# An attention and spectral-filter kernel on one core: stores and branch-matrix loads move from GpSimd's queue to SyncE's, with a deeper prefetch and a re-ordered hand-over

## The chip, the core and the metric

The kernel runs on one core of a Trainium2 chip. The core has TensorE (PE, the matrix engine, with its weight loads listed as PEld), VectorE (DVE), ScalarE (ACT), GpSimd (POOL) and SyncE (SP), which only issues transfers. Sixteen DMA engines move data between the core's memory and DRAM. They serve a queue of SP, one of ACT and one of GpSimd. The metric is the device time of one execution in microseconds (us); lower is better. The median of three runs is 2086.2 us (2082.62 to 2087.38).

## The reference, cut to what matters

Two images `x` of 128 channels by 64 x 64 pixels pass two layers, all in float32.

```python
x = x + conv_block(group_norm(x))          # layer 0: 7x7 neighbourhood attention, small linear maps
t = to_tokens(x)                           # (2, 4096, 128)
q = ln(t)
sim = q @ q.T / sqrt(128);  sim[diag] = -1e9
t = t + softmax(sim) @ q                   # layer 1a: attention over each block of tokens
u = ln(t)
# layer 1b ("ffn"): 16 causal filters phi, applied to u and to u with alternating signs,
# times the matrices sum over branches of w_i * M_plus[i], M_minus[i] (each 16 x 128 x 128),
# scaled by sigma**0.25, plus three short lags with M_u
t = t + spectral(u, sigma, phi, M_plus, M_minus) + short_lags(u, M_u)
```

The branch weights `w_i` come from a softmax over four values, and they are the same for all tokens.

## The kernel before, in words

The work runs in five stages, which follow each other on TensorE. Times are those of the profile.

1. **Layer 0**, to 347 us, for both images.
2. **Attention of image 0** (`attention(0, fill)`, L902), 347 to about 788 us.
3. **Attention of image 1** (`attention(1, fill)`), about 788 to 1262 us.
4. **A hand-over**, 1262 to 1314 us, in which the last token chunks of image 1 are finished.
5. **The ffn in frequency space** (`burst`, `project`, `mixed_bins`, `back`, `finished`), 1314 us to the end.

*Attention.* The 4096 tokens of an image are cut into eight chunks of 512. `pairs` (L913) is the list of the 36 chunk pairs, and each pair takes four steps. In a step TensorE makes one 128 x 512 block of scores for the pair that comes next (`weights`, L927), ScalarE takes its exponential (L932), and TensorE multiplies the current block with the tokens of one side (L1054, into the bank `other`). The other side of a pair needs the block transposed. For that the four blocks of a pair, 1 MB, are stored in DRAM by ACT's queue (`sent`, L956, `eb<-e`), loaded back by SP's queue in four pieces of 256 KB (`moved`, L963, `et<-eb`), turned by VectorE in 32 x 32 squares (`turned`, L972) and multiplied (`pair_onto`, L982). The distances are in steps: `MOVE` = 2 for the load, `TURN` = 7 for the turn, `DELAY` = 8 for the multiplication. There are two buffers for `et` and four for `eb`. VectorE must add `other` into `xa` (L1063) before TensorE can start the next pair, because `other` is one bank.

*Filling.* At the end of each step `fill` (L1381) takes one piece of other work from two lists of Python generators. `urgent` holds the chunks whose attention is complete: `after(b, c)` (L1087) normalises a chunk, multiplies it with the transform `tr`, copies the result out on ScalarE (L1128, `uo`), forms sums and differences on GpSimd (L1131, `ub`) and stores them in the DRAM tensor `us` by GpSimd's queue (L1135 and L1140). A chunk makes 16 stores, in three consecutive pieces. `steps` holds the rest: during image 0 the end of layer 0, the branch weights, the filters (`filters`, L1302), whose sums (L1357), negations (L1368) and stores to `gs` (L1332) are all GpSimd's, and the tokens of image 1 (`tokens`, L219); during image 1 `for_ffn` (L1457), which runs `filter_matrices` (L1274), loads `inv` and loads the first four filter blocks (`load_blocks`, L1448).

*`filter_matrices`.* 32 loads of 256 KB (`branch`, L1268, tile `st`, two buffers), each issued by GpSimd one piece ahead of its use. VectorE multiplies each with its branch weight and adds it into `mpl` or `mmi` (L1286, L1288). After every eight loads VectorE forms a difference and a sum (L1294, L1295), and GpSimd scales 8 slices of 128 x 128 by `sigma` (L1298, L1299).

*Order.* From the moment when the buffers of image 1 exist (L1043), the instructions of PE, DVE, ACT and POOL in attention stay in the order in which the program writes them (`manual_schedule`, L1044). SP's stay in the framework's scheduled order, except the four loads of `moved`, which keep their program order. All engines take their queues in order: a waiting instruction holds up everything behind it on its engine.

*Hand-over.* After attention of image 1 what is left in `urgent` is run generator by generator (L1488 to L1493), now with the sums on VectorE and the stores on SP (`adder`, L1484). Some pieces of the short lags (`kept`, L1193, L1209) are mixed in. Then the first four `ut` inputs of the ffn are loaded from `us` (`inputs`, L1520, L1675), and TensorE begins the first `burst` (L1542).

Of the kernel before, what the change touches and what calls it, by code (L numbers as in the profile page):

```python
# [8 lines left out]
F32 = mybir.dt.float32  # L9
# [93 lines left out]
def kernel(  # L103
# [773 lines left out]
    with ap_:  # L877
# [24 lines left out]
        def attention(b, fill):  # L902
# [14 lines left out]
            def weights(a, c, k, left, halves):  # L917
# [32 lines left out]
                    nc.vector.tensor_copy(e[:, 0:lo], pt[:, 0:lo])  # L950
                return e

            def sent(eh):

                eb = dram.tile([P, 4, 512], F32, tag="eb", name="eb", bufs=4)
                nc.scalar.dma_start(out=eb.rearrange("p q r -> p (q r)"), in_=eh)  # L956
                return eb

            def moved(eb):

                et = ep.tile([P, 4, 512], F32, tag="et", name="et", bufs=2)
                for q in range(4):
                    tc.keep_in_program_order(nc.sync.dma_start(  # L963
                        out=et[32 * q : 32 * q + 32], in_=eb[:, q].rearrange("(h p) r -> p h r", h=4)
                    ))
                return et

            def turned(et):

                for q in (0, 2):  # L970
                    flat = et[:, q : q + 2].rearrange("p q r -> p (q r)")
                    tc.keep_in_program_order(nc.vector.transpose(flat, flat))  # L972

            def turned_here(et, es, m):

# [59 lines left out]
            for i, (a, c) in enumerate(pairs):  # L1035
                following = pairs[i + 1] if i + 1 < len(pairs) else None
                coming, halves = [], []
                if a != c:
                    other = ps_o.tile([P, 512], F32, tag="other", name="other")
                else:  # L1040
                    owns[a] = ps_o.tile([P, 512], F32, tag="own", name="own", bufs=2)
                for j in range(4):
                    if tt[1] is not None and not ordered:  # L1043
                        ordered.append(written.enter_context(tc.manual_schedule(engines={engines.PE, engines.DVE, engines.Activation, engines.Pool})))  # L1044
                    if following:
                        coming.append(coming_of(*following, j, coming, halves))
# [35 lines left out]


        spare = [tok[0][:, 0:4, :]]
        adder = [nc.gpsimd, nc.gpsimd]

        def after(b, c):  # L1087

# [35 lines left out]
            def store(pu, n, r0, m, ri):  # L1124

                for s in range(2):
# [5 lines left out]
                    for sgn in range(2):  # L1132
                        to = us[r0 : r0 + m, sgn, :, 2 * hh + s, 2 * fp : 2 * fp + 2, b, par, :]
                        if ri is not None:
                            adder[1].dma_start(  # L1135
                                out=to[:, ri], in_=ub[:, sgn, :].rearrange("p (f d) -> p f d", d=P)
                            )
                            continue
                        for f in range(2):
                            adder[1].dma_start(  # L1140
                                out=to[:, :, f].rearrange("k i d -> i k d"), in_=ub[64 * f : 64 * f + 64, sgn, 0:P]
                            )

            for r0, c0 in row_tiles:
                for ri in range(2):
# [68 lines left out]
        def branch_weights():  # L1214
# [38 lines left out]

            yield
            mu2 = mu.rearrange("p k e -> p (k e)")
            loaded = [branch(m_u, i, nc.sync) for i in range(2)]
            yield
            for i in range(NBR):
                st = loaded.pop(0)
                if i == 0:  # L1260
                    nc.vector.tensor_scalar(mu2, st, wt[:, 0:1], None, ALU.mult)
                else:
                    nc.vector.scalar_tensor_tensor(mu2, st, wt[:, i : i + 1], mu2, ALU.mult, ALU.add)
                yield
                if i + 2 < NBR:
                    loaded.append(branch(m_u, i + 2, nc.sync))

        def branch(src, i, eng):  # L1268

            st = sp.tile([P, 4, P], F32, tag="st", name="st")[:, 0 : src.shape[1]]  # L1270
            eng.dma_start(out=st, in_=src[i].rearrange("k d e -> d k e"))
            return st.rearrange("p k e -> p (k e)")

        def filter_matrices(mpl, mmi):  # L1274

            parts_ = [(k0, dst, src, i) for k0 in range(0, KF, 4) for dst, src in ((mpl, m_plus), (mmi, m_minus)) for i in range(NBR)]
            loaded = [branch(m_plus[:, 0:4], 0, nc.gpsimd)]
            yield
            for at, (k0, dst, src, i) in enumerate(parts_):
                if at + 1 < len(parts_):  # L1280
                    k1, _, src1, i1 = parts_[at + 1]
                    loaded.append(branch(src1[:, k1 : k1 + 4], i1, nc.gpsimd))
                st = loaded.pop(0)
                dst2 = dst[:, k0 : k0 + 4].rearrange("p k e -> p (k e)")
                if i == 0:
# [4 lines left out]
                if dst is mpl or i + 1 < NBR:  # L1290
                    continue
                a, d = (m[:, k0 : k0 + 4, :].rearrange("p k e -> p (k e)") for m in (mpl, mmi))
                s = sp.tile([P, 512], F32, tag="st", name="mdiff")
                nc.vector.tensor_tensor(s, a, d, ALU.subtract)  # L1294
                nc.vector.tensor_tensor(a, a, d, ALU.add)  # L1295
                for k in range(4):
                    ks = slice(k * P, (k + 1) * P)
                    nc.gpsimd.tensor_scalar(a[:, ks], a[:, ks], sg[:, k0 + k : k0 + k + 1], None, ALU.mult)  # L1298
                    nc.gpsimd.tensor_scalar(d[:, ks], s[:, ks], sg[:, k0 + k : k0 + k + 1], None, ALU.mult)  # L1299
                yield  # L1300

        def filters():  # L1302
# [24 lines left out]
            def store(src, r0, n, ri, s, i, o):  # L1327
# [1 line left out]
                    gs.tensor, gs.offset + r0 * 4 * SG * GROW + (i * SG + s) * GROW + o * LL,  # L1329
                    [[4 * SG * GROW, n], [2 * SG * GROW, 2], [1, LL]],  # L1330
                )
                nc.gpsimd.dma_start(out=to, in_=src)  # L1332

            everything = [(r0, c0 + ri * P, (ri,), P) for r0, c0 in row_tiles for ri in range(2)]
            everything.append((left_row, left_col, (0, 1), 64))
# [41 lines left out]
        def filler(b, steps, kept=None):  # L1377
# [3 lines left out]
            def fill(c=None):  # L1381
                if c is not None:
# [7 lines left out]
                        urgent.append(lags)  # L1390
                    return

                for queue in (urgent, steps):
                    while queue:
                        got = next(queue[0], False)
# [31 lines left out]
        for gen in steps:  # L1427
            for _ in gen:
                pass
        mpl, mmi, inv, mu1, ctp = [None] * 5  # L1430

        def blocks(q):

# [11 lines left out]

        first_blocks = []

        def load_blocks():  # L1448
            for q in range(4):
                first_blocks.append(blocks(q))  # L1450
                yield

        def for_lags():
# [2 lines left out]

        def for_ffn():  # L1457

            nonlocal mpl, mmi, inv, mu1, ctp
            while spare != [None]:  # L1460
                yield True
            first_.close()
# [4 lines left out]
            inv = l1.tile([P, K2 // BC * 4 + 1, CQ], F32, name="inv")  # L1467
            ctp = ctx.enter_context(tc.tile_pool(name="blocks", bufs=5))
            nc.gpsimd.tensor_copy(mu1, mu)
            yield from filter_matrices(mpl, mmi)  # L1470

            nc.sync.dma_start(out=inv, in_=nc.inline_tensor(t_out, "t_out").ap().rearrange("(a p) c -> p a c", p=P))
            for s, (lo, hi) in enumerate(((0, CQ // 8), (CQ // 8, CQ // 4), (CQ // 4, CQ // 2), (CQ // 2, CQ))):
# [7 lines left out]
        kept = []  # L1481
        fill, left = filler(1, steps, kept)
        attention(1, fill)
        adder[:] = nc.vector, nc.sync  # L1484
        for gen in steps:
            for _ in gen:
                pass
        for gen in left:  # L1488
            for i, got in enumerate(gen):
                if got or gen is left[-2] and i < 2:  # L1490
                    next(kept[0], None)
        for _ in kept[0]:
            pass  # L1493
        lags = kept[1]
# [9 lines left out]
    with ExitStack() as cv:  # L1504
# [11 lines left out]
        def lag_bank():  # L1516
            used[0] += 1
            return sums(used[0] % 4)

        def inputs(b, q):  # L1520

            ut = cp.tile([P, 2, P], F32, tag="ut", name="ut")
            nc.sync.dma_start(
                out=ut.rearrange("p s d -> p (s d)"),
                in_=us[2 * q : 2 * q + 2, :, :, :, :, b].rearrange("g n i r f s d -> (g n i r f) (s d)"),
            )
            return ut

        TK = FB * KF
        KG = 4  # L1530
# [143 lines left out]
        to_load = list(order_)  # L1674
        ahead = [(ct, inputs(*to_load.pop(0))) for ct in first_blocks]  # L1675
        rest = []
        with tc.manual_schedule(engines={mybir.EngineType.PE}):
            y = new_y()
# [154 lines left out]
```

## Time and profile before

| | |
|---|---|
| median of three runs | 2086.2 us |
| the profiled execution: time, span | 2088.9 us, 2087.2 us |
| mean granted TensorE clock | 0.964 of full speed |
| GpSimd's queue (software): packets, MB | 18432, 33.50 MB, 5.6% of the 16 engines' span |
| SP's queue: packets, MB | 210674, 131.38 MB, 26.3% |
| ACT's queue: packets, MB | 8126, 58.04 MB, 7.0% |
| stores to `us` issued by GpSimd | 108 of 128 KB, 104 of 32 KB |
| loads of `st` issued by GpSimd | 32 of 256 KB |

The profile is one execution, with all times counted from its first instruction. A group row gives the busy time of an instruction group, its mean length and the idle time of the engine just before it, with what ended that idle time (the releaser). A windows row gives, for one stretch, the busy time of PE, PEld, DVE, ACT and POOL with the number of instructions, then the clock that TensorE was granted, the mean busy share of the DMA engines and the GB/s moved. A timeline row gives start and length of one or a few merged instructions, and in brackets the idle time before them and the releaser. Matrix products are listed in two halves each, so a count of 2 is one 128 x 512 product.

### The profile page before, as it was taken

To read this page: it belongs to the slowest core of one execution; us is meant where nothing else is said; L and a number is where in the kernel's file an instruction comes from. 1 tells how busy PE (TensorE), PEld (TensorE's weight loads), DVE (VectorE), ACT (ScalarE), POOL (GpSimd) and SP (SyncE) were. 2 spreads that over 40 slices of the span, in tenths; PEclk is the share of its full clock that TensorE was granted. 3 is DMA by queue.
4 is the path that set the end of the run, shared out by engine and by line. 5 is a ranking of instruction groups with operands and counts; after the bars stand their busy time and mean duration, and the time that the engine had idled before them with its cause. 6 is when DMAs were issued, how large, how long until landed. Compare 5 with 4: busy or idle time off the path is not lost.

```text
span 2087.2 us, 50881 instructions
## 1 busy us (share of the span) xinstructions
PE 1928.9 (92%) x20504; PEld 1358.8 (65%) x20504; DVE 944.7 (45%) x2918; ACT 722.5 (35%) x1686; POOL 780.4 (37%) x1262
## 2 busy tenths in 40 slices
PE   6899998999699998997869997899999999999998
PEld 4677775444244444443324444699999899999987
DVE  5799986542444343342524435333333334333332
ACT  3789885322132323221112222222222222222222
POOL 3467986308544337305344341022222122222211
PEclk9999999999899999998979998999999999999999
DMA  4222221677366534647666632222222123222211
GB/s 151 60 61 61 62 59 43 196 181 237 109 173 180 146 106 149 170 142 193 192 167 186 167 109 72 71 68 66 67 67 63 49 57 102 67 67 67 67 43 42
DMA packets 237466, 226.16 MB, mean 108 GB/s; under 512 B 129887, under 2 KB 193007, under 8 KB 229808
## 3 DMA queue, kind: packets, MB, share of 16 engines
q1 hardware_dynamic: 210674, 131.38, 26.3%
q10 hardware_dynamic: 8126, 58.04, 7.0%
q0 software_dynamic: 18432, 33.50, 5.6%
q8 instruction: 163, 2.67, 0.5%
q14 instruction: 71, 0.58, 0.1%
HBM read 131.40 MB, written 91.25 MB: 107 GB/s over the span
## 4 chain that ended last, share of the span: by engine, by line
PE 42%; DMA 3%; issue 3%; POOL 3%; DVE 2%; ACT 0%; SPq 0%; DVEq 0%; POOLq 0%; ACTq 0%
PE acc L1561 27%; PE pc L1542 7%; PE own L982 3%; PE bank L927 1%; DMA st<-in_m_plus_dram 1%; PE other L1054 1%; DMA st<-in_m_minus_dram 1%; PE pc L1600 1%; POOL ub L1131 1%; PE pc L1613 0%; PE bank L936 0%; PE bank L1150 0%; DMA ct<-gs 0%; PE pc L1642 0%; POOL mpl L1298 0%
## 5 line engine op out<-in xcount | busy, mean ns | idle before, releaser
L1547 DVE COPY y<-pc 128x512 f32<-128x512 f32 x320 | 206.0, 686 | 351.9 <-PE pc L1542 351.3
L1561 PE MATMUL acc<-y,mpl 32*128 32x256 f32 x5120 | 324.0, 379 | 0.9 <-DVE af L1571 0.9
L1561 PE MATMUL acc<-y,mmi 32*128 32x256 f32 x5120 | 316.5, 375 | 0.0
L1547 ACT COPY y<-pc 128x512 f32<-128x512 f32 x320 | 171.8, 589 | 400.9 <-PE pc L1542 396.3
L1561 PEld LDWEIGHTS acc<-y,mpl 32*128 32x128 f32 x5120 | 289.3, 186 | 8.6 <-DVE af L1571 1.7
L1561 PEld LDWEIGHTS acc<-y,mmi 32*128 32x128 f32 x5120 | 290.9, 185 | 3.9
L1572 POOL TENSOR_TENSOR af<-af 128x512 f32<-128x512 f32 x39 | 49.8, 1276 | 594.7 <-DVE af L1571 594.7
L982 PE MATMUL own<-et,tok 128*128 128x512 f32 x448 | 221.1, 617 | 42.3 <-DVE et L972 37.5
L1054 PE MATMUL other<-e,tok 128*128 128x512 f32 x448 | 232.9, 602 | 6.4 <-DVE xa L1063 6.4
L932 ACT ACTIVATE e<-bank 128x512 f32<-128x512 f32 x216 | 128.6, 600 | 298.9 <-PE bank L927 298.8
L927 PE MATMUL bank<-cm 128*128 128x512 f32 x432 | 226.1, 605 | 0.0
L1542 PE MATMUL pc<-ct,ut 32*128 32x256 f32 x2560 | 214.5, 380 | 6.0 <-DMA ut<-us 4.1
L982 PEld LDWEIGHTS own<-et,tok 128*128 128x128 f32 x448 | 85.9, 197 | 157.1 <-issue 100.5
L1542 PEld LDWEIGHTS pc<-ct,ut 32*128 32x128 f32 x2560 | 174.4, 188 | 12.5 <-issue 5.9
L1131 POOL TENSOR_TENSOR ub<-uo 128x256 f32<-128x256 f32 (+1 forms) x160 | 99.3, 647 | 132.1 <-ACT uo L1128 130.7
L1054 PEld LDWEIGHTS other<-e,tok 128*128 128x128 f32 x448 | 82.2, 193 | 99.4 <-issue 83.8
L972 DVE STREAM_TRANSPOSE et<-et 128x1024 f32<-128x1024 f32 x108 | 127.6, 1219 | 33.2 <-DMA et<-eb 31.4
L174 POOL TENSOR_TENSOR ln_rs<-ln_rs,mhalf 128x4 f32<-128x4 f32 x24 | 24.8, 1032 | 268.5 <-DVE ln_rs L173 268.4
L927 PEld LDWEIGHTS bank<-cm 128*128 128x128 f32 x432 | 76.8, 194 | 73.4 <-issue 66.1
L546 ACT ACTIVATE p<-p,mn 128x196 f32<-128x196 f32 x256 | 114.4, 449 | 13.2 <-DVE mn L536 12.6
L1128 ACT COPY uo<-bank 128x512 f32<-128x512 f32 (+1 forms) x96 | 46.8, 517 | 141.5 <-PE bank L1150 80.0
L943 ACT ACTIVATE e<-bank 128x512 f32<-128x512 f32 (+1 forms) x72 | 32.5, 457 | 152.0 <-DVE bank L941 151.9
(267 smaller groups left out, 2773.9 us busy)
## 6 DMA issues: line engine op xcount, KB each, us to landing
eb<-e ACTq DMA_DIRECT2D x54, 1024.0 KB
et<-eb SPq DMA_DIRECT2D x216, 256.0 KB
ut<-us SPq DMA_DIRECT2D x160, 128.0 KB
us<-ub POOLq DMA_DIRECT2D x108, 128.0 KB, 2.8
ct<-gs SPq DMA_DIRECT2D x320, 40.0 KB
vw<-vd SPq DMA_DIRECT2D x256, 49.0 KB
ct<-gs SPq DMA_DIRECT2D x320, 32.0 KB
vd<-v SPq DMA_DIRECT2D x128, 32.0 KB
```

The costliest lines, as they stand in the source:

```text
L546: nc.scalar.activation(p, p, AF.Exp, bias=t[name + "mn"][:, h : h + 1], scale=-1.0, accum_out=t["den"][:, u, h : h + 1],)
L927: nc.tensor.matmul(ps.rearrange("p (q t j) -> p q t j", q=4, t=4), lhsT=cm[b][:, n * P : (n + 1) * P], rhs=keys.rearrange("p (t q j) -> p ...
L932: nc.scalar.activation(e, ps.rearrange("p (q r) -> p q r", q=4), AF.Exp, bias=0.0, scale=ASCALE)
L972: tc.keep_in_program_order(nc.vector.transpose(flat, flat))
L982: nc.tensor.matmul(out_, lhsT=tok[b][:, n, :], rhs=e, start=first, stop=last, skip_group_check=True)
L1054: nc.tensor.matmul(turn(other, "p (q r) -> p q r"), lhsT=tok[b][:, n, :], rhs=es[j], start=(j == 0), stop=(j == 3),)
L1128: nc.scalar.copy(both[:, 0 : 2 * n], pu[s][:, 0 : 2 * n])
L1131: adder[0].tensor_tensor(ub[:, sgn, 0:n], both[:, 0:n], both[:, n : 2 * n], op)
L1542: nc.tensor.matmul(pcs[j].rearrange("p (g o c) -> p o g c", g=4, o=2)[:, :, at], lhsT=ut[rows_, par, :], rhs=cv_[rows_], start=True, stop= ...
L1547: (nc.scalar.copy if j % 2 else nc.vector.tensor_copy)(y[:, :, :, 4 * kl + j, :], pcs[j].rearrange("p (g x k) -> p k g x", g=4, k=KF))
L1561: nc.tensor.matmul(acc[j][:, 0:256], lhsT=(mmi if l else mpl)[rows_, k, :], rhs=y[rows_, k, 2 * l : 2 * l + 2].rearrange("p s n x -> p (s ...
L1572: eng.tensor_tensor(af[:, 0:2], af[:, 0:2], af[:, 2:4], ALU.add)
```

## The change

- In attention SP joins the engines whose order is the program's. `in_place` replaces the explicit request for order where that holds already.
- All stores to `us` and `gs` are put on a list (`behind_`). `stores()`, called at the start of each `fill`, issues what the previous piece has put there, on SP. GpSimd issues no store and no load in these stages.
- `filter_matrices` loads three pieces ahead instead of one. The loads are SP's, and alternate between two pairs of buffers (a pool `mix` with two is added to the two of `sp`). The difference tile uses another buffer (`uo`). The scaling by `sigma` moves from GpSimd to ScalarE.
- The first four `ut` inputs are loaded with the first four filter blocks, during attention of image 1, into a pool of four buffers of their own.
- In the hand-over two chunks at a time are advanced in turn, one piece of each, with the stores behind them and one piece of the short lags per round.

```diff
+            def in_place(ins):
+                return ins if ordered else tc.keep_in_program_order(ins)
...
-                    tc.keep_in_program_order(nc.sync.dma_start(
+                    in_place(nc.sync.dma_start(
...
-                        ordered.append(written.enter_context(tc.manual_schedule(engines={engines.PE, engines.DVE, engines.Activation, engines.Pool})))
+                        ordered.append(written.enter_context(tc.manual_schedule(engines={engines.PE, engines.DVE, engines.Activation, engines.Pool, engines.SP})))
...
-        adder = [nc.gpsimd, nc.gpsimd]
+        adder = [nc.gpsimd]
+        behind_ = []
+
+        def stores():
+            while behind_:
+                to, src = behind_.pop(0)
+                nc.sync.dma_start(out=to, in_=src)
...
-                            adder[1].dma_start(
-                                out=to[:, ri], in_=ub[:, sgn, :].rearrange("p (f d) -> p f d", d=P)
-                            )
+                            behind_.append((to[:, ri], ub[:, sgn, :].rearrange("p (f d) -> p f d", d=P)))
...
+        def branch(src, i, pool=None):
+            st = (pool or sp).tile([P, 4, P], F32, tag="st", name="st")[:, 0 : src.shape[1]]
+            nc.sync.dma_start(out=st, in_=src[i].rearrange("k d e -> d k e"))
...
-            loaded = [branch(m_plus[:, 0:4], 0, nc.gpsimd)]
-            yield
-            for at, (k0, dst, src, i) in enumerate(parts_):
-                if at + 1 < len(parts_):
-                    k1, _, src1, i1 = parts_[at + 1]
-                    loaded.append(branch(src1[:, k1 : k1 + 4], i1, nc.gpsimd))
+            to_come = iter(enumerate(parts_))
+            loaded = []
+            def load():
+                for at, (k0, _, src, i) in to_come:
+                    loaded.append(branch(src[:, k0 : k0 + 4], i, pool if at % 4 > 1 else None))
+                    return
+            for _ in range(3):
+                load()
+                yield
+            for k0, dst, src, i in parts_:
+                load()
                 st = loaded.pop(0)
...
-                s = sp.tile([P, 512], F32, tag="st", name="mdiff")
+                s = sp.tile([P, 512], F32, tag="uo", name="mdiff", bufs=2)
...
-                    nc.gpsimd.tensor_scalar(a[:, ks], a[:, ks], sg[:, k0 + k : k0 + k + 1], None, ALU.mult)
-                    nc.gpsimd.tensor_scalar(d[:, ks], s[:, ks], sg[:, k0 + k : k0 + k + 1], None, ALU.mult)
+                    for to, of in ((a, a), (d, s)):
+                        nc.scalar.activation(
+                            to[:, ks], of[:, ks], AF.Identity, bias=0.0, scale=sg[:, k0 + k : k0 + k + 1]
+                        )
...
-                nc.gpsimd.dma_start(out=to, in_=src)
+                behind_.append((to, src))
...
+                stores()
                 for queue in (urgent, steps):
...
-                first_blocks.append(blocks(q))
+                first_blocks.append((blocks(q), inputs(0, q)))
...
-            yield from filter_matrices(mpl, mmi)
+            with tc.tile_pool(name="mix", bufs=2) as mixp:
+                yield from filter_matrices(mpl, mmi, mixp)
+            utp = ctx.enter_context(tc.tile_pool(name="inputs", bufs=4))
...
-        for gen in left:
-            for i, got in enumerate(gen):
-                if got or gen is left[-2] and i < 2:
-                    next(kept[0], None)
+        *chains, residuals = left
+        while chains:
+            for gen in chains[:2]:
+                if next(gen, 0) == 0:
+                    chains.remove(gen)
+                stores()
+            next(kept[0], None)
+        for _ in residuals:
+            next(kept[0], None)
```

More of the change, by code (lines that the diff above doesn't have):

```diff
@@ L971, in turned @@
                     flat = et[:, q : q + 2].rearrange("p q r -> p (q r)")
-                    tc.keep_in_program_order(nc.vector.transpose(flat, flat))
+                    in_place(nc.vector.transpose(flat, flat))
             def turned_here(et, es, m):
@@ L1134, in store @@
                         if ri is not None:
-                            adder[1].dma_start(
-                                out=to[:, ri], in_=ub[:, sgn, :].rearrange("p (f d) -> p f d", d=P)
-                            )
+                            behind_.append((to[:, ri], ub[:, sgn, :].rearrange("p (f d) -> p f d", d=P)))
                             continue
                         for f in range(2):
-                            adder[1].dma_start(
-                                out=to[:, :, f].rearrange("k i d -> i k d"), in_=ub[64 * f : 64 * f + 64, sgn, 0:P]
-                            )
+                            behind_.append((to[:, :, f].rearrange("k i d -> i k d"), ub[64 * f : 64 * f + 64, sgn, 0:P]))
             for r0, c0 in row_tiles:
@@ L1255, in branch_weights @@
             mu2 = mu.rearrange("p k e -> p (k e)")
-            loaded = [branch(m_u, i, nc.sync) for i in range(2)]
+            loaded = [branch(m_u, i) for i in range(2)]
             yield
@@ L1265, in branch_weights, with filter_matrices @@
                 if i + 2 < NBR:
[L1266 to L1271, printed above, removed]
+                    loaded.append(branch(m_u, i + 2))
+        def branch(src, i, pool=None):
+            st = (pool or sp).tile([P, 4, P], F32, tag="st", name="st")[:, 0 : src.shape[1]]
+            nc.sync.dma_start(out=st, in_=src[i].rearrange("k d e -> d k e"))
             return st.rearrange("p k e -> p (k e)")
-        def filter_matrices(mpl, mmi):
+        def filter_matrices(mpl, mmi, pool):
             parts_ = [(k0, dst, src, i) for k0 in range(0, KF, 4) for dst, src in ((mpl, m_plus), (mmi, m_minus)) for i in range(NBR)]
-            loaded = [branch(m_plus[:, 0:4], 0, nc.gpsimd)]
-            yield
-            for at, (k0, dst, src, i) in enumerate(parts_):
-                if at + 1 < len(parts_):
-                    k1, _, src1, i1 = parts_[at + 1]
-                    loaded.append(branch(src1[:, k1 : k1 + 4], i1, nc.gpsimd))
+            to_come = iter(enumerate(parts_))
[9 more added lines that the diff above has]
+                load()
                 st = loaded.pop(0)
@@ L1429 @@
                 pass
-        mpl, mmi, inv, mu1, ctp = [None] * 5
+        mpl, mmi, inv, mu1, ctp, utp = [None] * 6
         def blocks(q):
@@ L1446, with inputs @@
         first_blocks = []
+        def inputs(b, q):
+            ut = utp.tile([P, 2, P], F32, tag="ut", name="ut")
+            nc.sync.dma_start(
+                out=ut.rearrange("p s d -> p (s d)"),
+                in_=us[2 * q : 2 * q + 2, :, :, :, :, b].rearrange("g n i r f s d -> (g n i r f) (s d)"),
+            )
+            return ut
         def load_blocks():
             for q in range(4):
-                first_blocks.append(blocks(q))
+                first_blocks.append((blocks(q), inputs(0, q)))
                 yield
@@ L1457, in for_ffn @@
         def for_ffn():
-            nonlocal mpl, mmi, inv, mu1, ctp
+            nonlocal mpl, mmi, inv, mu1, ctp, utp
             while spare != [None]:
@@ L1483 @@
         attention(1, fill)
-        adder[:] = nc.vector, nc.sync
+        adder[:] = [nc.vector]
         for gen in steps:
@@ L1518, in lag_bank @@
             return sums(used[0] % 4)
[L1520 to L1527, printed above, removed]
         TK = FB * KF
@@ L1673 @@
         order_ = [(b, q) for b in range(NB) for q in range(K2)]
-        to_load = list(order_)
-        ahead = [(ct, inputs(*to_load.pop(0))) for ct in first_blocks]
+        to_load = order_[len(first_blocks) :]
+        ahead = list(first_blocks)
         rest = []
```

## The prediction

> **What bounds the kernel now.** I read the page first: the busy rows and the slices.
>
> ```profile
> PE 1928.9 (92%) x20504; PEld 1358.8 (65%) x20504; DVE 944.7 (45%) x2918; ACT 722.5 (35%) x1686; POOL 780.4 (37%) x1262
> PE   6899998999699998997869997899999999999998
> PEclk9999999999899999998979998999999999999999
> DMA  4222221677366534647666632222222123222211
> ```
>
> TensorE is the bound nearly everywhere. Only where its digit falls can this change gain: slice 10, slices 18 to 20, 24. In all three the clock falls too, and in the middle one the DMA engines are at 6 to 7 tenths. The windows of these stretches give what is missing (after the window's length: PE, PEld, DVE, ACT, POOL busy, clock, DMA share, GB/s):
>
> ```profile
> 533.00:551.00 18.00, 0.55 (x4) 0.42 (x3) 0.97 (x4) 0.00 (x0) 14.81 (x21) 0.56 0.20 44
> 788.00:801.00 13.00, 7.70 (x47) 4.70 (x44) 2.49 (x9) 4.44 (x10) 11.76 (x18) 0.76 0.23 73
> 956.00:1106.00 150.00, 104.94 (x262) 45.74 (x261) 59.64 (x100) 23.67 (x43) 57.88 (x86) 0.84 0.67 177
> 1262.00:1314.00 52.00, 34.84 (x170) 18.94 (x168) 27.49 (x104) 13.84 (x25) 7.91 (x10) 0.86 0.30 88
> 1314.00:2087.00 773.00, 756.86 (x13286) 727.43 (x13286) 263.70 (x470) 213.22 (x428) 166.12 (x390) 0.99 0.24 64
> ```
>
> The ffn (last row) has PE busy 98% and is not touched. TensorE lacks 45 us in 956 to 1106, 17 in the hand-over, 17 and 5 in the first two. The timeline names the causes. First GpSimd and TensorE at 533 to 551:
>
> ```profile
> 544.91 1.58 POOL L1332 DMA_DIRECT2D gs<-fb  x3 [0.29 <-POOL fb L1357]
> 546.56 1.49 POOL L1368 TENSOR_SCALAR fn<-fb 32x512 f32<-32x512 f32 x1
> 548.34 0.55 POOL L1332 DMA_DIRECT2D gs<-fn  x1 [0.29 <-POOL fn L1368]
> 548.95 1.04 POOL L174 TENSOR_TENSOR ln_rs<-ln_rs,mhalf 128x4 f32<-128x4 f32 x1
> 550.52 1.15 PE L202 MATMUL bank<-ident,tok 128*128 128x128 f32 x4 [17.45 <-DVE tok L191]
> ```
>
> The power (L174), ready to run since 529, stands behind GpSimd's filter pieces, of some 5.7 us each, of which 2.1 are issuing stores. Then 956 to 973:
>
> ```profile
> 955.95 1.56 POOL L1271 DMA_DIRECT2D st<-in_m_plus_dram  x2
> 964.96 0.49 DVE L1286 TENSOR_SCALAR mpl<-st,wt 128x512 f32<-128x512 f32 x1 [16.95 <-DMA st<-in_m_plus_dram]
> 965.74 0.75 POOL L1271 DMA_DIRECT2D st<-in_m_plus_dram  x1 [8.22 <-DMA st<-in_m_plus_dram]
> 969.83 2.36 DVE L972 STREAM_TRANSPOSE et<-et 128x1024 f32<-128x1024 f32 x2
> 972.25 3.66 PE L982 MATMUL own<-et,tok 128*128 128x512 f32 x4 [14.67 <-DVE et L972]
> ```
>
> VectorE waits for a branch matrix issued one step before; its turns (L972) stand behind that, and TensorE behind them. Last, the end of the hand-over:
>
> ```profile
> 1310.02 2.46 SPq L1523 DMA_DIRECT2D ut<-us  x5
> 1313.88 2.09 PE L1542 MATMUL pc<-ct,ut 32*128 32x256 f32 x16 [4.10 <-DMA ut<-us]
> ```
>
> **Part 1: three loads ahead, on SP.** TensorE's four gaps here are 14.67, 7.65, 15.22 and 5.31 us, all released through VectorE after `st`: 42.9 us. The clock is at half for 47.8 us around them, by the trace's clock records. The Trainium skill (TensorE: Matmul & The Clock Gate, section "HAM oscillation — how this bites in real kernels") prices that at half the throttled time, 24 us. But in 27.7 of the 47.8 us TensorE had no work at all; only 20 us of work ran at half speed, so the row gives 10 us, and I take that. Gap and clock: 53 us at most. TensorE's own work in the 150 us is then 104.9 - 10 = 95.
>
> What is late next is the DMA engines. Their share of 0.67 over 150 us is 100 us of work. By packet records from 950 to 1110: `et` 40 us, `eb` 23, GpSimd's queue (32 `st` and a chunk's stores) 36, `ct` and `inv` 5.5, which now move behind this stretch. On SP's queue the 8.4 MB of `st` are 16384 packets of 512 B. Such packets took 28 ns in the quiet hand-over and 44 to 52 ns beside `et`: over 16 engines 29 to 53 us; the chunk's stores 5 to 9. Together 97 to 125 us against TensorE's 95. The Trainium skill (DMA: Bandwidth & Descriptors, "Issuing engines are not separate DMA queues") speaks against the move: all queues share the same engines, and a second issuer saves only issue time. By it the move gains nothing and `st` now stands behind `et` in one queue. The rows agree that bandwidth is short (0.83 to 0.87 at 975 to 1050), but the gaps are mostly latency: after the first load the DMA share falls to 0.4 while one load at a time is fetched. So I credit the depth, not the queue. Three steps are 3 x 2.58 = 7.7 us (three products of 0.86 us a step) against a landing of 3.6 us median, 10.7 worst. I take 107 us for the stretch, near the middle of 97 and 125: **43 us** gained (ends 25 and 53).
>
> The scaling on ScalarE: 8 activations a group by the nearest row (128x128 from memory, 0.49 us) are 3.9 us in ACT's queue, four times, with the next exponentials behind them. ACT was busy 24 of 150 us and works three steps ahead, so I take 0; at a diagonal pair, where TensorE waits for ACT, up to 4 us each. Better than 0 is possible: GpSimd's 0.61 us each leave its queue. The loads cost SP about 0.4 us each to issue (`m_u` rows), beside 1.8 us per four `et`.
>
> **Part 2: GpSimd issues nothing.** A chunk's stores cost GpSimd 8 x 0.73 + 8 x 0.67 = 11.2 us, the sums 8 x 0.735 + 8 x 0.465 = 9.6. On most of the path they are beside a full TensorE (24 to 25 of 25 us busy from 800 to 950 and 1110 to 1260) and gain nothing. They gain at three places. The filters: 4 pieces with two sums (1.5 us) and 8 with sums and a negation (3.1 us) are 31 us without issuing, in place of 55. The power at 549 could then come at 531. But a store is now issued a piece later, its buffer (four, two per piece) comes free only on landing (5.0 us median), and GpSimd and SP wait for each other: two pieces per 2.7 + 1 + 5 us, or 4.4 us each, is 35 us for the eight. I leave a gap of 5 us (ends 0 and 12): 17.45 + 2.6 at half clock - 6 = 14. At 667 a gap of 2.52 us with 1.7 of clock has the same cause: 3.5. At the start of image 1 (788 to 801) TensorE waits for `uo` copies that wait for GpSimd: gaps of 5.3 us and 3 of clock, 6.5 gained; 522 gives 1. **25 us** (10 to 33).
>
> What it costs: SP now waits for GpSimd's sums in order, and behind it stand `et` loads, the following `st` and later `ct`. A piece's four sums (2.9 us) fit a step of about 3 us, so SP is one step late. Loaded at step 2 and turned at 7, `et` has five steps, 12.9 us, of which issue and transfer take about 7. The trace of before shows no such wait. It costs between 0 and 15 us; as SP has 6 us of room, I take **4**.
>
> **Part 3: the hand-over.** With two chunks side by side the last chunk's statistics run before the other's 8 differences, not after. In the changed order VectorE's queue from 1266.5 on holds two chunks of 4.5 us (statistics, scaling) and 4.3 (sums), 2.6 left of an earlier one, and 8.4 of short lags: 28.6 us where it took 44.5. Following it by hand, the last chunk's `z` comes at 1288.5 rather than 1292.6: 4 us. Early inputs take away the 4.10 us wait for `ut` (its cover: `ut` 0 to 3 land a hundred us before; the fifth is needed four bursts later). The first burst then finds a warm clock: 16 half products took 2.09 us at 1313.9 and 1.15 at 1324.4; with the lags between them 4 us. **12 us** (6 to 18). The wait of SP for landed stores before the first early `ut` (about 4.6 us) lies within the `et` room.
>
> **The sum.** 43 + 25 + 12 - 4 = 76 us. The profiled run of 2088.9 us would be 2013; against the median, 2.7 us lower, **2010**.
>
> **Rivals.** *Everything goes*: 53 + 33 + 18 = 104, 1982 us. For it: DMA needs as little as 97 us, and `et` may slip. Against: two resources would have to be full at once; the best 20 us of the trace had a DMA share of 0.93. *DMA-bound*: `st` behind `et` in one queue, 25 + 12 + 10 - 5 = 42, 2044 us. For it: 44 to 52 ns a packet beside `et`. It shows as a DMA share over 0.9 with VectorE still waiting for `st`. *Slower*: SP held up at every chunk. Once SP reaches an `et` load over 6 us late, each further us is a gap of TensorE. With 16 chunks the 80 us of gain are eaten from 5 us more, that is 11 us late per chunk, about 2100 us at 12. For it: in the filters SP may be 17 us late by the 4.4 us pieces. Against: ordinary pieces take 2.9 us of GpSimd. *It does nothing*: the waits return under other names with the same length, 2086.
>
> **How the numbers follow.** Forecast (1995 to 2028) 0.61, everything goes 0.14, DMA-bound 0.18, slower 0.05, nothing 0.02. The range takes in both cases of gain with their bounds: 1982 to 2044, leaving out some 2 in 10 beyond the ends, in the slower case and in the nothing case. About 0.2% (4 us) is what a measurement of this kernel can tell from no change: faster 0.93, same 0.02, slower 0.05.
>
> **What would show it.** In the changed profile: no POOL DMA row after image 1's input; TensorE's wait before L202 in tokens under 8 us; in the stretch of `mpl` and `mmi` PE digits of 9, DMA share over 0.85, VectorE's waits for `st` (four rows of the waits, 71 us together) down to about 10; no PE wait for `ut`; the ffn still 773 us. Wrong would be: SP's own waits for `ub` or `fb` with PE waits for `et` behind them, or `st` waits that stay at DMA shares below 0.7.

## The result, and the profile after

The changed kernel takes 2059.3 us (median; 2054.5 to 2062.0), the kernel before 2085.9 us on the same chip: ratio 0.9872, 95% interval 0.9848 to 0.9896. That is 26.5 us faster, where 76 were forecast; the direction was right, two thirds of the gain did not come. The profiled execution took 2061.6 us (span 2059.8).

The busy rows and slices of the page:

```profile
PE 1924.6 (93%) x20504; PEld 1355.8 (66%) x20504; DVE 941.0 (46%) x2918; ACT 733.1 (36%) x1718; POOL 570.6 (28%) x954
PE   6899998999899999897978898999999999999998
PEclk8999999999999999999989999999999999999999
DMA  5222221667656534648865632222222123222211
```

GpSimd has 308 instructions and 210 us less, as the change says. Slice 10 of TensorE, counted from 0, has filled (6 to 8). The hole at slices 18 to 20 (7, 8, 6 before) is still there: slice 18 and slices 20 to 22 have 7, 7, 8, 8. The same stretches in windows, shifted to where they lie now and the third taken as 210 us (length, then PE, PEld, DVE, ACT, POOL, clock, DMA share, GB/s):

```profile
527.00:545.00 18.00, 12.03 (x29) 5.55 (x29) 7.81 (x19) 2.65 (x5) 12.00 (x14) 0.81 0.48 112
778.00:791.00 13.00, 11.51 (x57) 5.96 (x56) 5.84 (x24) 6.23 (x13) 8.07 (x13) 1.00 0.33 98
945.00:1155.00 210.00, 165.83 (x443) 74.18 (x442) 81.17 (x148) 49.66 (x106) 17.32 (x26) 0.89 0.71 187
1249.00:1290.00 41.00, 34.36 (x165) 19.08 (x164) 25.15 (x99) 13.67 (x25) 4.90 (x6) 0.88 0.32 95
```

Three of the four did what was forecast. In the third TensorE still lacks 44 us, at a clock of 0.89. The kernel before, over 210 us from the start of that stretch:

```profile
956.00:1166.00 210.00, 163.12 (x434) 72.24 (x433) 81.95 (x148) 39.62 (x72) 81.82 (x123) 0.89 0.66 178
```

At a DMA share of 0.71 the 16 DMA engines are not full. Of the two signs by which the prediction wanted to be found wrong, the first has come: SP's own waits for `ub`, with waits for `et` behind them (below). The second, `st` waits that stay at DMA shares below 0.7, has not quite: the share is 0.71, and the `st` waits fell by a third. In one table, with what TensorE lacks (in the first row that one gap, in the third its gaps of over 2.5 us, in the others the windows' missing busy time; us):

| place | before | forecast | after | best version below |
|---|---|---|---|---|
| power before the tokens of image 1 (one gap) | 17.45 | 5 | 4.81 | 4.71 |
| start of image 1 | 5.3 | about 2 | 1.5 | 1.5 |
| rest of image 1's attention | 42.9 | about 10, clock included | 44.8 | 10.5 |
| hand-over | 17.2 | about 5 (12 less) | 6.6 | 9.2 |

What VectorE waits for in attention and hand-over (line and tile, releaser, total us, times, longest), first in the kernel before, then in the changed one:

```profile
DVE et L972 <- DMA et<-eb: 31.4, 10, 5.6
DVE mpl L1288 <- DMA st<-in_m_plus_dram: 21.9, 5, 8.6
DVE mmi L1286 <- DMA st<-in_m_minus_dram: 21.2, 4, 17.5
DVE mpl L1286 <- DMA st<-in_m_plus_dram: 16.9, 1, 16.9
DVE mmi L1288 <- DMA st<-in_m_minus_dram: 10.7, 9, 2.4
```

```profile
DVE et L975 <- DMA et<-eb: 66.3, 14, 14.1
DVE mpl L1299 <- DMA st<-in_m_plus_dram: 18.2, 1, 18.2
DVE mmi L1299 <- DMA st<-in_m_minus_dram: 17.7, 1, 17.7
DVE mpl L1301 <- DMA st<-in_m_plus_dram: 9.1, 2, 4.8
DVE inv L1501 <- DMA inv<-t_out: 8.0, 1, 8.0
```

The many waits for `st` (71 us in four rows) have shrunk to 45 us in three, 36 of it in two long waits, and the waits for `et` have doubled. A queue ahead of both is late. SP's own waits name it:

```profile
SPq L1094 <- POOL ub L1141: 164.8, 91, 23.6
SPq L1094 <- DMA eb<-e: 81.8, 14, 9.6
```

L1094 is the store in `stores()`, here of sums to `us`. The first row was forecast: SP waits for GpSimd's sums. The second was not. A store of `us` has nothing to do with `eb`, the chunk of exponentials that ScalarE stores; yet SP stood 82 us for it. The timeline shows one such place, then the two that follow it, in SP, VectorE and TensorE:

```profile
1022.31 1.75 SPq L966 DMA_DIRECT2D et<-eb  x4
1024.15 20.16 SPq L1094 DMA_DIRECT2D us<-ub  x12
1044.37 1.65 SPq L1277 DMA_DIRECT2D st<-in_m_minus_dram  x3
1046.12 1.88 SPq L966 DMA_DIRECT2D et<-eb  x4
1048.31 0.49 DVE L1299 TENSOR_SCALAR mmi<-st,wt 128x512 f32<-128x512 f32 x1 [17.74 <-DMA st<-in_m_minus_dram]
1051.13 3.78 PE L985 MATMUL own<-et,tok 128*128 128x512 f32 x4 [12.44 <-DVE et L975]
...
1092.38 0.43 SPq L1499 DMA_DIRECT2D inv<-t_out  x1
1099.03 0.98 DVE L1501 TENSOR_SCALAR inv<-inv,seg 128x80 f32<-128x80 f32 x4 [7.96 <-DMA inv<-t_out]
1102.34 2.92 PE L985 MATMUL own<-et,tok 128*128 128x512 f32 x3 [6.85 <-DVE et L975]
...
1146.87 3.78 PE L985 MATMUL own<-et,tok 128*128 128x512 f32 x4 [7.16 <-DMA ct<-gs]
```

Twelve stores occupy SP for 20.2 us; the matrices and the `et` load that VectorE and TensorE are waiting for are behind them. The instruction records tell why. Each DMA issue names the completion counter that it will raise, and SP first waits for that counter's last user. From the records of these 20 us (engine, start in us, transfer, counter):

```
ScalarE 1028.20  eb<-e   raises 107
SP               wait for 107, over at 1033.74
SP      1033.79  us<-ub  raises 107
ScalarE 1038.50  eb<-e   raises 105
SP      1042.40  us<-ub  waits for 105, raises 105
```

SP and ScalarE take eight counters (100, 102 to 108) in turn, in the order of the program. So one of the eight transfers after each chunk store has that store's counter and must wait until its 1 MB has landed: the last raise of 107 by the first chunk comes at 1033.72 us, and SP's store starts at 1033.79. Of the 81.8 us, 10.4, 12.5 and 11.7 fall at the three chunks before TensorE's gaps of 6.9, 11.5 and 12.4 us. Before, the `us` stores were GpSimd's, whose transfers have eight other counters (111 to 118), and SP's loads of `et` had their data from `eb` to wait for anyhow.

**Theory A** (SP's queue): what is missing is lost because `st` and `et` loads stand in one queue behind stores, above all behind stores that wait on ScalarE's chunk stores through a shared counter. **Rival B** (bandwidth): the stretch is bound by the bytes and pieces that the DMA engines move; where they are issued doesn't matter.

### The profile page after: what moved, and what is told of

Read it like the earlier page. It is cut to its first block, busy times and chain, and to the rows that moved or that the text cites. A ratio compares the mean times of both kernels' runs of the same rounds, so it can differ in the third digit from the quotient of the medians.

```text
span 2059.8 us, 50961 instructions
## 1 busy us (share of the span) xinstructions
PE 1924.6 (93%) x20504; PEld 1355.8 (66%) x20504; DVE 941.0 (46%) x2918; ACT 733.1 (36%) x1718; POOL 570.6 (28%) x954
## 4 chain that ended last, share of the span: by engine, by line
PE 75%; DVE 8%; DMA 5%; POOL 4%; issue 4%; ACT 1%; SPq 1%; DVEq 0%; POOLq 0%; ACTq 0%
PE acc L1584 27%; PE own L985 10%; PE bank L927 7%; PE pc L1565 7%; PE other L1057 6%; PE bank L349 2%; PE bank L559 2%; PE bank L202 2%; PE bank L1156 2%; DMA et<-eb 2%; PE bank L1199 1%; DMA eb<-e 1%; DVE et L975 1%; PE bank L523 1%; PE po L581 1%
## 5 line engine op out<-in xcount | busy, mean ns | idle before, releaser
L985 PE MATMUL own<-et,tok 128*128 128x512 f32 x448 | 225.9, 629 | 61.2 <-DVE et L975 49.1
```

What stands on the lines that cost most here:

```text
L985: nc.tensor.matmul(out_, lhsT=tok[b][:, n, :], rhs=e, start=first, stop=last, skip_group_check=True)
```

## The experiments

The times of before beside these runs were 2082.7, 2084.9, 2083.7 and 2082.7 us. Differences are between medians of runs. These come from different chips; taken by the ratios to before on the same chip, the gains over after are up to 4 us smaller (run 2: 21 us instead of 24).

**1. Stores back on GpSimd.** The kernel after with

```diff
-                nc.sync.dma_start(out=to, in_=src)
+                nc.gpsimd.dma_start(out=to, in_=src)
```

in `stores()`.

> The changed kernel, but the stores of us and gs are issued by GpSimd's queue again (still one piece behind the sums); the branch matrices stay on SP, three ahead. Theory A (counters): every transfer of SP and ACT waits for the transfer that last used its completion counter, and SP and ACT share eight of them, so a store stood still until a later 1 MB store of e had landed. GpSimd has eight others. Then SP's waits of a us store for e (82 us) are gone, TensorE's gaps at 823, 950 and 1039 (31 us, and some 8 of half clock) are gone, and the gap before the tokens of image 1 comes back (about 13 us more, as GpSimd issues again): about 2033 us. Theory B (bandwidth): et is late because the DMA engines are full with the branch matrices in front of it; then those gaps stay and only the tokens' gap is added: 2065 to 2075 us.

Measured 2045.1 us, ratio 0.9819 (0.9796 to 0.9843): 14 faster than after, where B expected a loss, but 12 short of A's number. Where after has gaps of 11.5 and 12.4 us at the branch matrices, none is over 3.2. The tokens' gap comes back with the stores on GpSimd, as A's number allowed for. What is short lies elsewhere: four gaps of 2 to 3 us stay at the branch matrices (10.4 us together), and the hand-over with the first burst behind it, whose stores this edit puts on GpSimd too, has gaps of 5.4, 2.5 and 4.8 us where after has 3.0 and 2.3. The tokens' gap in this kernel's timeline:

```profile
546.13 1.15 PE L202 MATMUL bank<-ident,tok 128*128 128x128 f32 x4 [15.29 <-DVE tok L191]
```

So taking the stores from GpSimd is right for that gap (10 us); giving them to SP costs more than that elsewhere.

**2. Only the chunk stores moved.** The kernel after with

```diff
-                nc.scalar.dma_start(out=eb.rearrange("p q r -> p (q r)"), in_=eh)
+                nc.gpsimd.dma_start(out=eb.rearrange("p q r -> p (q r)"), in_=eh)
```

The 54 stores have the same 1 MB in pieces of the same 8192 B; they now raise GpSimd's counters.

> The changed kernel, but the 1 MB stores of e (eb) are issued by GpSimd's queue instead of ACT's; order of SP and all stores as in the changed kernel. The same bytes, the same places. Theory A (counters): SP's stores no longer share a counter with eb; their waits for eb go from 82 us to near 0, TensorE's gaps at 602, 823, 950 and 1039 (34 us and some 8 of half clock) go: about 2018 us; the gaps at 1095 and 1140 (inv, ct and ut ahead of et) stay. Theory B (bandwidth, or the order on SP alone): nothing changes, 2055 to 2065 us.

Measured 2035.4 us, ratio 0.9773 (0.9751 to 0.9796): 24 faster than after; B, which expected no change, falls. SP's row of 81.8 us is gone from its waits, and the same twelve stores take half the time. The timeline of this kernel:

```profile
997.17 11.05 SPq L1094 DMA_DIRECT2D us<-ub  x12
1008.27 2.13 SPq L1277 DMA_DIRECT2D st<-in_m_minus_dram  x3
1010.50 3.76 SPq L966 DMA_DIRECT2D et<-eb  x4
1015.61 2.92 PE L985 MATMUL own<-et,tok 128*128 128x512 f32 x3 [5.25 <-DVE et L975]
```

A burst of 11 us where the forecast gave `et` 6 us of room leaves a gap of 5; with 9 us more of waits (20.2 against 11.05) it was 12.4. A's number was missed by 17 us: of the gaps at the chunk stores two remain, of 4.4 and 5.3 us, and the gap behind the load of `inv` grew from 6.9 to 12.4. That ScalarE was set free is not the reason for the gain: in after ScalarE waited at its chunk stores only for its own exponentials (24.5 us in all 54), never for a transfer.

**3. The three-ahead loads alone**, in GpSimd's queue: the kernel before with `filter_matrices` as in after (four buffers, the difference in `uo`), its loads issued by GpSimd.

```diff
-            loaded = [branch(m_plus[:, 0:4], 0, nc.gpsimd)]
+            for _ in range(3):
+                load()
+                yield
...
-                s = sp.tile([P, 512], F32, tag="st", name="mdiff")
+                s = sp.tile([P, 512], F32, tag="uo", name="mdiff", bufs=2)
```

> The kernel before with one part of the change: the branch matrices are loaded three pieces ahead in four buffers, still by GpSimd's queue. Theory A (a wait of latency, which depth hides; the loss in the changed kernel is from SP's counters): VectorE's waits for the branch matrices fall from 71 us to under 25 and the stretch of mpl and mmi gains 30 to 43 us: about 2050 us. Theory B (bandwidth): the waits move to et, gain under 15 us, over 2070 us.

Measured 2055.2 us, ratio 0.9862 (0.9842 to 0.9881): 27.5 us of gain, nearer A's number, though under its 30 to 43. Two of the four gaps are gone; those of 10.5 and 11.0 us that remain wait for the first load of a group, 17.3 and 16.3 us, and are issued at 953.6 and 1042.0 us, when GpSimd has got through a chunk's sums and stores.

**4. The hand-over alone**: the kernel before with the two chunks side by side and the early `ut` (from the end of the diff).

```diff
-                first_blocks.append(blocks(q))
+                first_blocks.append((blocks(q), inputs(0, q)))
...
+        while chains:
+            for gen in chains[:2]:
+                if next(gen, 0) == 0:
+                    chains.remove(gen)
+            next(kept[0], None)
```

> The kernel before with only the last part of the change: two chunks side by side in the hand-over and the first four ut loaded during attention. If the stage's gain is this part's own (10.6 us in the hand-over, 3.5 at the start of the ffn): about 2072 us. If it came from the stores behind the sums, or is paid for by the early ut in SP's queue during attention: 2078 us or more.

Measured 2072.5 us, ratio 0.9951 (0.9932 to 0.9970): 10 us gained, as forecast (12).

**5. The order at the end of image 1.** What was left in run 2 was a gap of 12.4 us with VectorE waiting for `inv`, and one of 5.2 behind the first blocks. Run 2 with

```diff
+            nc.sync.dma_start(out=inv, in_=nc.inline_tensor(t_out, "t_out").ap().rearrange("(a p) c -> p a c", p=P))
             nc.gpsimd.tensor_copy(mu1, mu)
...
-                first_blocks.append((blocks(q), inputs(0, q)))
+                for ct in block_parts(q):
+                    yield
+                first_blocks.append((ct, inputs(0, q)))
                 yield
```

where `block_parts` yields after each pair of transfers, and the old load of `inv` is gone.

> The kernel after with the chunk stores on GpSimd's queue (as in the earlier run of 2035.4 us), the inverse table's load moved ahead of the branch matrices, and the first blocks' loads cut into pieces, at most two transfers to a fill. Queue theory (what is left at the end of image 1 is the order of SP's and VectorE's queues: VectorE stood 13.5 us for the table, which the turn had to wait behind, and the turn stood behind a whole block's loads): the gaps of 12.4 and 5.2 us go, with 2 to 5 us of half clock behind the long one: 2013 to 2020 us. Bandwidth theory (the stretch is bound by what the 16 DMA engines move): the bytes are the same, so 2030 us or more.

Measured 2013.0 us (2012.4 to 2014.0), ratio 0.9656 (0.9642 to 0.9671). Both gaps are gone, the bytes are the same. This is the best version of all, 3.4% faster than before and 46 us faster than after. Its window of the stretch that was 165.83 of 210 us in after:

```profile
920.00:1130.00 210.00, 191.65 (x555) 86.93 (x553) 93.74 (x181) 60.20 (x125) 33.20 (x53) 0.98 0.80 216
```

**6. Stores split by image.** Run 5 with the stores of the sums on GpSimd during image 1's attention.

```diff
+        storer[0] = nc.gpsimd
         attention(1, fill)
+        storer[0] = nc.sync
```

> The run above, with the stores of the sums on SP during image 0's attention and on GpSimd's queue during image 1's. Issue-time theory (a burst of 12 stores takes SP 10.9 us, 5 more than the room of the et load behind it): the two gaps of 4.4 and 5.2 us at the branch matrices go too, and the tokens' gap of image 0 stays away: 2001 to 2009 us. Rival (GpSimd, which waits in order for ScalarE's exponentials before each chunk store, holds the stores and so the sums' buffers up): no gain over the run above, 2013 us or more.

Measured 2026.0 us, ratio 0.9719 (0.9704 to 0.9733): 13 slower than run 5; the rival is right that nothing is gained. Its wait is the reverse of the one that was expected: not the stores behind the chunks but the chunks behind the stores. GpSimd and SP in this kernel's timeline:

```profile
1012.23 5.30 POOL L1095 DMA_DIRECT2D us<-ub  x8
1017.53 0.59 POOL L959 DMA_DIRECT2D eb<-e  x1
...
1023.70 2.81 SPq L966 DMA_DIRECT2D et<-eb  x4
1026.62 0.39 SPq L1278 DMA_DIRECT2D st<-in_m_minus_dram  x1
```

The chunk is stored late, SP waits up to 13.0 us for it at `et`, and the `st` behind it is late too (VectorE waited 12.2 us, TensorE 9.4).

**7. The stores on SP alone**: the kernel before with the store part of the change (`behind_`, `stores()`, SP in the written order); branch matrices still on GpSimd and, as in before, one piece ahead of their use (the expectation's "two ahead" counts the loads that are under way).

```diff
-                            adder[1].dma_start(
-                                out=to[:, ri], in_=ub[:, sgn, :].rearrange("p (f d) -> p f d", d=P)
-                            )
+                            behind_.append((to[:, ri], ub[:, sgn, :].rearrange("p (f d) -> p f d", d=P)))
```

> The kernel before, with only the stores of the sums and of the filters moved from GpSimd to SP, one fill behind; branch matrices still two ahead on GpSimd. The prediction's working for this part: gaps of 25 us go and 4 come, 2065 us. Theory of the shared counters and of issue time: the tokens' gap goes (12 us), but SP's et loads now stand behind bursts of 12 stores and behind chunk stores of ScalarE, which costs 5 to 12 us at several chunks: 2073 to 2088 us.

Measured 2058.9 us, ratio 0.9881 (0.9863 to 0.9899): 26 us faster than before. Here A's expectation was wrong, and the prediction's 21 us nearly right, though not for its reason. The tokens' gap went from 17.45 to 4.67 us (13). SP stands 86.7 us for `eb` here too, and pays: gaps of 7.6, 3.4 and 2.8 us at chunks that had none over 1.3 us in before. But at the branch matrices the gaps fell from 42.9 to 24.7 us, with the loads no deeper than before: VectorE's longest wait for one is 9.8 us instead of 17.5. GpSimd, rid of its stores, issues them sooner. So a wait of SP costs little by itself; it costs where other work that is needed soon is queued behind it.

**8. The branch matrices off SP**: the kernel after with

```diff
-            nc.sync.dma_start(out=st, in_=src[i].rearrange("k d e -> d k e"))
+            (nc.gpsimd if pool_st[0] else nc.sync).dma_start(out=st, in_=src[i].rearrange("k d e -> d k e"))
```

(`pool_st[0]` is true from `filter_matrices` on).

> The kernel after, with only the branch-matrix loads (three ahead, four buffers, as in after) put on GpSimd's queue. It tells which of the transfers behind SP's waits is the one that costs. If the st loads are it (VectorE stood 45 us for them): 2035 to 2042 us, and the waits for et stay harmless. If the et loads are late for the same reason: VectorE's 66 us of waits for et stay, the long gaps at two chunks shrink by some us only, 2046 to 2054 us. Bandwidth theory: 2056 us or more.

Measured 2052.8 us, ratio 0.9841 (0.9823 to 0.9858), some 6 us faster than after by medians, though the intervals overlap. The gaps at two chunks shrank from 11.5 and 12.4 us to 7.9 and 5.9; SP still stands 86.6 us for `eb`, VectorE 87 us for `et`. So both cargoes are hurt, `et` more lastingly.

**9. Fewer stores** (192 instead of 256 in the whole kernel). Run 5 with one store for both signs of a sum.

```diff
-                            behind_.append((to[:, ri], ub[:, sgn, :].rearrange("p (f d) -> p f d", d=P)))
+                        to = us[r0 : r0 + m, :, ri, 2 * hh + s, 2 * fp : 2 * fp + 2, b, par, :]
+                        behind_.append((to, ub.rearrange("p s (f d) -> p s f d", d=P)))
```

> The run of 2013.0 us (chunk stores on GpSimd's queue, inverse table early, first blocks in pieces), with one store for both signs of a sum instead of two, the same bytes and pieces. A store takes SP 0.9 us and a burst of them 10.9 us. If the time is per issue, a burst shrinks to 6 or 7 us and the two gaps of 5.6 and 4.8 us left at the branch matrices go: 2001 to 2007 us. If it is per piece of the transfer, one store takes 1.7 us or more and nothing is gained: 2011 to 2016 us.

Measured 2015.7 us, ratio 0.9679 (0.9652 to 0.9706): no gain over run 5, and the two gaps stay (5.4 and 5.2 us). The edit reaches only the stores of 128 KB, so one burst went from twelve issues in 10.9 us to ten in 10.8. By issues alone it should have been 1.8 us shorter, so the time does not go with their number; that it goes with the pieces is argued from this one burst. Some of run 5's burst is waiting: 2.1 us for counters that SP's own `et` loads had taken, and 1.4 for the sums.

**10. Order alone**: the kernel after with the edits of run 5 to `inv` and the first blocks, chunk stores on ScalarE's queue.

```diff
+            nc.sync.dma_start(out=inv, in_=nc.inline_tensor(t_out, "t_out").ap().rearrange("(a p) c -> p a c", p=P))
             nc.gpsimd.tensor_copy(mu1, mu)
...
+                for ct in block_parts(q):
+                    yield
```

> The kernel after with only the inverse table's load early and the first blocks' loads in pieces; chunk stores stay on ScalarE's queue. If this saving adds to that of the chunk stores' move (it was 22 us beside it, 2035.4 to 2013.0), 2036 to 2041 us. If the pieces only fall behind other waits of SP's stores for ScalarE's chunk stores, which stay, 2045 to 2056 us.

Measured 2045.0 us, ratio 0.9821 (0.9799 to 0.9844): 14 us, at the edge of the second expectation. Of the four long gaps the two late ones (6.9 and 7.2 us) shrank to one of 2.3; the two behind the chunk stores stay (12.7 and 12.1 us). The two repairs are worth 24 and 14 us alone and 46 together.

**11 and 12. The depth of before**, in the kernel after and in run 5:

```diff
-            for _ in range(3):
+            for _ in range(1):
```

The first matrix is loaded one piece before its use, and each use is preceded by one more load. So these runs load one piece ahead, as before does, and not three; the "two" of the expectations counts the loads that are under way, and "the third one" stands for the two that are added.

> The kernel after with the branch matrices loaded two ahead instead of three, still by SP and in the same four buffers. By the prediction's working depth is what the 43 us come from: 2080 us or more. By the theory that SP's queue decides when they are issued, the third one ahead brings nothing here, and the table of inverses comes two fills earlier, away from a turn: 2050 to 2062 us.

> The run of 2013.0 us (chunk stores on GpSimd's queue, inverse table early, first blocks in pieces), with the branch matrices two ahead instead of three. On SP's queue as it is in after the third one ahead brought nothing. If that was because the waits for chunk stores swallowed it, it is worth something here, where they are gone: 2022 us or more. If the loads come when SP's queue gets to them, however many are allowed, it is worth nothing here either: 2010 to 2017 us.

Run 11 took 2057.3 us, ratio 0.9883 (0.9857 to 0.9909): no difference from after that can be told. Its gaps at the two chunks are 15.0, 2.5 and 12.3 us rather than 11.5 and 12.4, so the depth does earn 6; but it delays what follows by two fills, and these put `inv` and the blocks where they cost 14.0 us of gaps, against 6.6 in run 11. Run 12 took 2023.9 us, ratio 0.9718 (0.9702 to 0.9735), 11 slower than run 5, with gaps of 10.1 and 10.0 us where run 5 has 5.6 and 4.8. So the deeper prefetch, which brings nothing that can be told in after, is worth 11 us once the queue is free. That is still far from 43.

## Why the prediction missed: two costs too small, and a gain put down to one part alone

**The failed step** is the cost in Part 2: "It costs between 0 and 15 us; as SP has 6 us of room, I take **4**." It was worked out from SP's wait for GpSimd's sums alone. The stores also stand behind ScalarE's chunk stores, by the shared counters: 10 to 12.5 us at each of the three chunks with the long gaps (6.9, 11.5 and 12.4 us), beyond the room at once. Taking this wait away was worth 24 us (run 2; 21 by the ratios), five to six times the 4, and beyond the bound of 15. I had even written the threshold down, in the slower rival ("Once SP reaches an `et` load over 6 us late, each further us is a gap of TensorE"), and gave it 0.05 because ordinary pieces take 2.9 us of GpSimd. The mechanism of that rival is what happened, at a few chunks and not at all sixteen.

**Second, what was costed at nothing.** Part 1 notes that `ct` and `inv` "now move behind this stretch" and gives that no price. In before SP's order in attention was not the program's, and `inv` was issued at 991.5 us, 127 us before VectorE scaled it (1118.6). With SP in the written order it is issued at 1092.4 where it stands, 6.6 us before its use, and the turn stands behind it: 6.9 us. Part 3 put the early `ut` "within the `et` room". In after three whole blocks of `ct` and `ut` take SP 9.5 us ahead of an `et` load (1127.2 to 1136.8 us; 1.8 of it `ut`), and a burst of stores with 4.2 us of wait for `eb` stands before them: VectorE waits 14.1 us for that `et`, and TensorE has a gap of 7.2 us (its row names a load of `ct`; the turn that it needs ends at 1146.8). Moving both was worth 14 us alone, and 22 beside run 2. The forecast of 2010 lacks these two terms: with both repaired the kernel takes 2013.0 us. That this is so near is in part chance: Part 1 gave all its 43 us to the depth.

**Part 1, 43 us.** That the gaps were not a matter of bandwidth is right: run 5 moves the same bytes there at a DMA share of 0.80, and TensorE is busy 192 of 210 us. "So I credit the depth, not the queue" is half wrong: what the depth brings depends on the queue. It was 27.5 us with GpSimd's stores ahead of the loads (run 3), 11 us on SP once the chunk stores' waits were gone (run 12), and nothing that can be told on SP as it is in after (run 11). Much of the four gaps came from GpSimd's stores ahead of the loads: with these gone the loads at the old depth save 18 us of gaps (run 7). The depth alone took 21 us from these gaps (run 3), the stores' move 18, and run 5, with both, 32, which is less than their sum. The Trainium skill (DMA: Bandwidth & Descriptors, "Issuing engines are not separate DMA queues") holds that all issuers share the same DMA engines and a second one saves only sequencer time. Of bandwidth the runs agree. But with the same bytes in the same pieces, the issuer of 54 stores decided over 24 us: SP's waits for these stores (81.8 us) went with it.

**Part 2, gains of 25 us.** The tokens' gap was forecast at 5 us and is 4.8; the start of image 1 went from 5.3 us missing to 1.5. Right, and run 1 shows the cause by bringing the gap back.

**Part 3, 12 us.** Run 4 gives 10 alone. Right, but for what the early `ut`, with the blocks, cost in SP's queue.

**The rivals.** *DMA-bound* (2044) came nearest by its number, and is refuted as a mechanism by run 2. *Everything goes* (1982) was not reached by any version.

**What stays open.** That each of the 24 us of run 2 is a counter's doing is not shown: moving the store changed its queue too, and there was no run that changed only the counter. Nor did a run have the stores on SP with SP's order left to the scheduler, so what the written order costs by itself, beyond `inv` and the first blocks, is not known. The two gaps of about 5 us in run 5 were not removed.

## What to carry to other kernels

Before a DMA is moved to another engine's queue, list for each transfer ahead of it what it can wait for, the counter that it shares with other engines' transfers included, and give the sum to whatever is needed soon behind it; compare with its room. If an engine is put into a written order, look for the loads that the scheduler had issued early, and write them early. And when two parts of a change shorten the same gaps, cost them together: 26, 27.5 and 10 us alone were 26.5 together here, and 72 once the two losses in SP's queue were repaired (run 5).

## What the runs showed of the hardware that was not expected

- In all these programs the transfers of SP and ScalarE raise the same eight completion counters (100, 102 to 108), and GpSimd's raise others (111 to 118): SP's stores stood 81.8 us for ScalarE's transfers in after, and not at all once GpSimd issued these (run 2).
- Issues slow down in a burst of small pieces. A store of `us` took SP 0.48 us to issue (median), and GpSimd 0.72 in before; within run 5's burst of twelve, all of 512 B pieces, single ones took up to 2.1 us, and the four `et` loads after run 2's burst took 3.76 us rather than 1.75. Ten issues of the same pieces took as long as twelve (run 9). Why an issue takes longer in a burst is not shown.
